# Attention scores on 32-row tiles with the last four dims in a float32r pass, values on 64-column tiles

## The chip, the cores and the metric

The kernel runs on one core of a Trainium2 chip. The metric is the device time of one execution in microseconds (us), the median of several runs.

## The reference

One block of a diffusion transformer on `x` of shape (2, 2048, 576), with a condition vector per batch; 16 heads of 36 dims, hidden layer of 2304. All of it is float32.

```python
mod = jax.nn.silu(c) @ w_ada + b_ada
sh_msa, sc_msa, g_msa, sh_mlp, sc_mlp, g_mlp = jnp.split(mod, 6, axis=1)
xn = _ln(x, 1e-06)
xn = xn * (1 + sc_msa[:, None, :]) + sh_msa[:, None, :]
qkv = (xn @ w_qkv + b_qkv).reshape(B, N, 3, H, hd)
q, k, v = (qkv[:, :, 0], qkv[:, :, 1], qkv[:, :, 2])
q = _ln(q, 1e-05, qn_g, qn_b)
k = _ln(k, 1e-05, kn_g, kn_b)
attn = jnp.einsum('bqhd,bkhd->bhqk', q, k) * scale
attn = jax.nn.softmax(attn, axis=-1)
o = jnp.einsum('bhqk,bkhd->bqhd', attn, v).reshape(B, N, C)
o = o @ w_proj + b_proj
x = x + g_msa[:, None, :] * o
xn2 = _ln(x, 1e-06)
xn2 = xn2 * (1 + sc_mlp[:, None, :]) + sh_mlp[:, None, :]
h = jax.nn.gelu(xn2 @ w1 + b1, approximate=False)
x = x + g_mlp[:, None, :] * (h @ w2 + b2)
```

## The kernel before

The work of one batch goes through three stages, and after both batches the MLP follows.

**Input stage** (`inputs`). For each of 16 tiles of 128 tokens: layer norm, transposes to features by tokens, the product with `w_qkv`, the bias (VectorE), the norm per head, and transposes of q and k back to features by tokens (`by_feature`). Their evictions fill `qo` (the first five 128-row chunks of the 1152 features of q and k) and `kr` (the other four); v stays tokens by features in `vt`, with a column of ones behind every head's 36 columns, so that the values product also sums the softmax's denominator. The contraction over 576 input features is four 128-row tiles (`whole`, line 351) and a rest of 64 rows, which is done for the two output halves side by side on 64-row tiles (`halved`, line 362). In this stage VectorE runs in the order written.

**Attention** (`attend`). Heads go in pairs p (8 of them), queries in blocks qb of 512 (4 of them), keys in chunks kc of 128 (16 of them). For every step (p, qb, kc):
- `scores` (line 900): the 36 dims of a head lie in a 64-row half of `kts[p % 2]` and of `qts`; the rest of the rows is zero. A chunk is cut into two halves of 64 keys, so that two heads times two halves make four products on 64x64 tiles of the TensorE array: keys stationary, 512 queries moving.
- ScalarE takes the exponential of the whole PSUM tile of 128 x 1024 (line 908), into `pt`. There is no maximum to subtract, since a bound on the scores is known from the norms' gains and biases.
- `values` (line 916): the same four tiles, with 64 of the chunk's keys as rows and 64 columns of `vt` as columns. Each of the two key halves has a PSUM bank of its own in `acc`.
- After the last chunk, `finish` adds the two banks (lines 928 and 929, VectorE), writes the row of denominators to DRAM and reads it back broadcast (lines 933 and 934), takes the reciprocal (935), multiplies (936), and puts the rows into `qo` (941), where they replace q.

The loop issues the scores of a step before the values of the step before, so that the exponential of a chunk runs beside TensorE's work on others. PSUM has two tiles of two banks for scores (`s`) and two for `acc`. q and k are brought from `qo` and `kr` to the tiles by SBUF to SBUF DMAs on SyncE's queue (`take_heads`, line 729): two or three for a block of q or a pair of k, as a head's 36 rows lie within one 128-row chunk or across two. There are three q tiles and two k tiles. Each engine's order is made by a scheduler from the program's order and dependencies, so that loads are issued well before the step in which they are written.

The first attention steps of a batch still hold the transposes of the last two token tiles (the hooks at kc 2 and 5 of the first block), whose keys the first block needs in its last four chunks.

**Output projection** (`outputs`) and the **MLP** follow; the change doesn't touch them.

The matmul of a float32 operand is shown in the profile as two records on TensorE (PE) and two weight loads (PEld).

Of the kernel before, what the change touches and what calls it, by code (L numbers as in the profile page):

```python
# [7 lines left out]

F32 = mybir.dt.float32
I32 = mybir.dt.int32  # L10
AF = mybir.ActivationFunctionType
# [10 lines left out]
FULL = 4  # L22
NKC = FULL + 1


@with_exitstack
def dit_block(
# [56 lines left out]
    def acc_tile():  # L84
        return psum["a"].tile([P, 2, 512], F32, tag="acc", name="acc")

# [351 lines left out]
    def attention(b, qk, vt):  # L438
# [4 lines left out]
        with tc.tile_pool(name=f"b1_{b}", bufs=1) as b1p, tc.tile_pool(name=f"b2_{b}", bufs=2) as b2p:  # L443
# [107 lines left out]
            for p in range(NPAIR):  # L551
                behind = None
                for s in range(steps):
                    qb, kc = divmod(s, NT)
                    if kc == 0:
                        qt = shifted_q(p, qb)
                    pt = scores(p, qt, kc)
                    if p + 1 < NPAIR:
                        largest(p + 1, s)
                    if behind is not None:  # L560
                        values(p, *behind)
                        if behind[2] == NT - 1:
                            finish(p, qb - 1, behind[0])
                    if kc == 0:
                        acc = acc_tile()[:, 0, :]
                    behind = (acc, pt, kc)
                    if p + 2 < NPAIR and qb == NBLK - 1 and kc % 2 == 1:
                        prepare(p + 2, kc // 2)
                values(p, *behind)
                finish(p, NBLK - 1, behind[0])  # L570
# [117 lines left out]

    def head_rows(first):

        at = first
        while at < first + HD:
            n = min(P - at % P, first + HD - at)
            yield at // P, at % P, at - first, n
            at += n

    def block_of_small():
# [16 lines left out]
        vv = vt[:, 0 : NT * H * HV].rearrange("p (t h e) -> p t h e", t=NT, h=H)  # L714
        kts = [kv.tile([P, N], F32, name=f"kt{i}") for i in range(2)]
        qts = [kv.tile([P, BLK], F32, name=f"qt{i}") for i in range(3)]
        for t in (*kts, *qts):
            nc.gpsimd.memset(t, 0.0)
        nc.gpsimd.memset(vv[:, :, :, HD : HD + 1], 1.0)
        nc.gpsimd.memset(vt[:, NT * H * HV :], 0.0)  # L720
        den_dram = dram.tile([B, NPAIR, NBLK, 2, BLK], F32, name="den_dram")

        def chunk(c, cols):
            return qo[:, c, cols] if c < NKC else kr[:, c - NKC, cols]

        def take_heads(dst, first, cols):
            for h in range(2):
                for c, row, d, n in head_rows(first + h * HD):
                    nc.sync.dma_start(
                        out=dst[64 * h + d : 64 * h + d + n, :], in_=chunk(c, cols)[row : row + n, :]  # L730
                    )

        def take_k(p, blk=None):
            cols = slice(0, N) if blk is None else slice(blk * BLK, (blk + 1) * BLK)
            take_heads(kts[p % 2][:, cols], C + p * 2 * HD, cols)

        def take_q(p, qb):
            cols = slice(qb * BLK, (qb + 1) * BLK)
            take_heads(qts[(p * NBLK + qb) % 3], p * 2 * HD, cols)

# [36 lines left out]
        def inputs(b, weights, work, xnt, loaded):  # L777

            wq, wq4, bq = weights
            normed, squares = {}, {}  # L780

# [32 lines left out]

            def by_feature(t, parts, all_on_vector=False):
                both = normed.pop(t)
                parts = [
                    parts[c // 8][:, c % 8 // 4, c % 4 * P : c % 4 * P + P] for c in range(NQK)
                ]
                for c, ps in enumerate(parts):  # L820
# [12 lines left out]
                if t % TPB == TPB - 1:  # L833
                    if t == TPB - 1:
                        take_q(0, 0)
                    take_k(0, t // TPB)

# [5 lines left out]
            for t in range(NT):  # L843
                both = work.tile([P, 2 * C], F32, name="both", bufs=3)
                for w in range(3):
# [25 lines left out]
                    if w == (1 if t % 2 == 0 else 0):  # L871
                        if t + 1 < NT:
                            ahead = input_by_feature(b, rows)
                        if t >= 2:
                            by_feature(t - 2, [s_tile(), s_tile()])
                        if t + 2 < NT:
                            rows = next_rows(t + 2)
# [7 lines left out]
                before, xnt = both, ahead  # L885
            return lambda t, spare: by_feature(t, [spare, s_tile()], True)

        def attend(b, pool, hooks):

            def scores(p, qb, kc):
                ps = s_tile()
                for c in range(2):
                    for h in range(2):
                        r = slice(64 * h, 64 * h + 64)
                        k0 = kc * P + 64 * c
                        nc.tensor.matmul(  # L900
                            ps[64 * c : 64 * c + 64, h, :],
                            kts[p % 2][r, k0 : k0 + 64],
                            qts[(p * NBLK + qb) % 3][r, :],
                            start=True,
                            stop=True,
                        )
                pt = pool.tile([P, 2, BLK], F32, name="pt", bufs=3)
                nc.scalar.activation(pt, ps, AF.Exp, scale=SCALE)  # L908
                return pt

            def values(p, acc, pt, kc):
                for h in range(2):
                    for c in range(2):
                        r = slice(64 * c, 64 * c + 64)
                        v0 = (kc * H + 2 * p + h) * HV
                        nc.tensor.matmul(  # L916
                            acc[64 * h : 64 * h + 64, c, :],
                            vt[r, v0 : v0 + 64],
                            pt[r, h, :],
                            start=(kc == 0),  # L920
                            stop=(kc == NT - 1),
                        )

            def finish(p, qb, acc):


                ot = pool.tile([P, BLK], F32, name="ot", bufs=2)
                nc.vector.tensor_copy(ot, acc[:, 0, :])  # L928
                nc.vector.tensor_tensor(ot, acc[:, 1, :], ot, ALU.add)
                den = pool.tile([P, BLK], F32, name="den", bufs=2)  # L930
# [13 lines left out]

            steps = [(p, qb, kc) for p in range(NPAIR) for qb in range(NBLK) for kc in range(NT)]
            behind = None
            for p, qb, kc in [*steps, (None, None, None)]:
                pt = None if p is None else scores(p, qb, kc)
                if (p, qb, kc) in hooks:
                    hooks[p, qb, kc]()  # L950
                if kc == 6 and (p, qb) != (NPAIR - 1, NBLK - 1):
                    take_q(*((p, qb + 1) if qb + 1 < NBLK else (p + 1, 0)))
                if kc == 8 and qb == 1 and p + 1 < NPAIR:
                    take_k(p + 1)
                if behind is not None:
                    bp, bqb, bkc, bpt = behind
                    if bkc == 0:
                        acc = acc_tile()
                    values(bp, acc, bpt, bkc)
                    if bkc == NT - 1:  # L960
                        finish(bp, bqb, acc)
                behind = (p, qb, kc, pt)

# [79 lines left out]
        for b in range(B):  # L1043
# [5 lines left out]
            close_psum()  # L1049
            close_psum = opened_psum(a=2, s=2)  # L1050
            opening = {}
# [24 lines left out]
            def output_opened():  # L1076
# [3 lines left out]
                (0, 0, 0): spare_taken,  # L1080
                (0, 0, 2): lambda: last_inputs(NT - 2, opening["spare"]),
                (0, 0, 5): last_inputs_done,
                (4, 0, 4): output_opened,
            }
            if b == 0:
                hooks |= {
                    (0, 2, 4): ada_opened,
                    (1, 0, 9): ada_gates,
                    (2, 0, 9): ada_feature_rows,
                    (2, 0, 12): ada_features,  # L1090
                }
# [40 lines left out]
        NB = B * NBLK  # L1132
        NG = BLK // PAIR
        gelus = [dram.tile([NG, P, NF, PAIR], F32, name=f"gelu{n}") for n in range(NB)]
        mx, close_mx = opened("mx")
# [176 lines left out]
        def hidden_loaded(q):  # L1312
            n, g = divmod(q, NG)
            nc.sync.dma_start(out=hidden[q % len(hidden)], in_=gelus[n][g])
# [32 lines left out]
        def second_product(q, gate, gate_bias):  # L1347
# [25 lines left out]
            for pair in ((3, 4), (2, 5), (6, 7), (1,)):  # L1373
# [15 lines left out]
                elif pair == (6, 7):  # L1389
                    nc.vector.tensor_tensor(c11, c11, ms[6], ALU.add)  # L1390
                    nc.vector.tensor_tensor(c00, c00, ms[7], ALU.add)
            if q + 3 < NB * NG:
                hidden_loaded(q + 3)
# [8 lines left out]
        for b in range(B):  # L1402
            gate, gate_bias = (hs.tile([P, C], F32, name=f"gate{i}") for i in range(2))
            for i, g in enumerate((gate, gate_bias)):
                nc.sync.dma_start(out=g, in_=gate_dram[2 + i, b, :].partition_broadcast(P))
            for q in range(b * NBLK * NG, (b + 1) * NBLK * NG):
                second_product(q, gate, gate_bias)
# [42 lines left out]
```

## Time and profile before

| | before |
|---|---|
| time, median of 3 | 3492.86 us (3491.9 to 3493.2) |
| span of the profiled execution | 3490.8 us |
| TensorE busy | 3439.7 us, 99% |
| ScalarE busy | 1495.4 us, 43% |
| VectorE busy | 1265.8 us, 36% |
| GpSimd busy | 260.4 us, 7% |
| attention, batch 0 and batch 1 | 265 to 1155 us and 1468 to 2352 us from the span's start |

A group of instructions in the profile is one line of the code, one engine, one operation and one shape. Behind the shapes stand the count, then the group's busy time in us and the mean length of one in ns, and then the idle time of that engine just before these instructions, with what ended most of it. Matmuls on different tiles of the array overlap, so the lengths of their records add to more than the time in which they ran; the distance between starts is what counts. In a timeline the columns are the start, the length of the merged run, the engine, the line, the operation, and the number of instructions; `64*64` is the rows and columns of the array that a matmul uses, and `64x512` its moving operand.

### The profile page before, as it was taken

What the parts mean: (1) busy time and instruction counts of PE and PEld (TensorE: products, weight loads), DVE (VectorE), ACT (ScalarE), POOL (GpSimd) and SP (SyncE); (2) the same over time, 40 slices, a digit from 0 to 9 for tenths busy, and PEclk for the clock granted to TensorE, in tenths of its full rate; (3) what the DMA queues carried; (4) which work ended last, traced back from release to release, by engine and by line L of the source; (5) the groups of instructions that cost most, each with busy time, mean ns of one, the idle gap of its engine ahead of it and who ended that gap; (6) DMA issues with size and microseconds to landing.
All of it is one profiled execution on the core that took longest, in us unless ns stands there. A gap on an engine that the chain in (4) does not pass through costs nothing.

```text
span 3490.8 us, 56258 instructions
## 1 busy us (share of the span) xinstructions
PE 3439.7 (99%) x24287; PEld 1945.6 (56%) x24287; DVE 1265.8 (36%) x1737; ACT 1495.4 (43%) x1928; POOL 260.4 (7%) x250
## 2 busy tenths in 40 slices
PE   8999999999999999999999999998999999999998
PEld 5773333333333677633333333336788788777776
DVE  4662112211121356611121211127445444455554
ACT  2335555555555133355555555551555454000000
POOL 2110000000000111100000000005000000011111
PEclk9999999999999999999999999999999999999999
DMA  3001211111100310011010010015422222433321
GB/s 121 28 21 53 68 50 28 34 29 37 38 22 23 122 36 25 20 46 27 27 29 29 23 28 27 21 37 192 139 99 84 84 86 71 166 122 126 117 104 35
DMA packets 105183, 215.98 MB, mean 62 GB/s; under 512 B 13988, under 2 KB 56557, under 8 KB 101869
## 3 DMA queue, kind: packets, MB, share of 16 engines
q1 hardware_dynamic: 93956, 174.19, 15.6%
q0 software_dynamic: 10240, 36.61, 3.0%
q8 instruction: 193, 3.16, 0.4%
q10 hardware_dynamic: 728, 1.48, 0.2%
q14 instruction: 66, 0.53, 0.1%
HBM read 125.96 MB, written 56.91 MB: 52 GB/s over the span
## 4 chain that ended last, share of the span: by engine, by line
PE 94%; DVE 2%; issue 2%; DMA 1%; ACT 0%; POOL 0%; SPq 0%; DVEq 0%; POOLq 0%; ACTq 0%
PE acc L916 25%; PE s L900 25%; PE s L1378 13%; PE s L351 13%; PE m L1228 11%; PE m L1242 2%; PE s L362 2%; PE one L1228 2%; PE s L821 1%; PE t L1287 1%; PE s L329 0%; DVE xt L259 0%; DMA gb_rows<-rows_dram 0%; DVE x L997 0%; DMA x_dram<-x 0%
## 5 line engine op out<-in xcount | busy, mean ns | idle before, releaser
L908 ACT ACTIVATE pt<-s 128x1024 f32<-128x1024 f32 x1024 | 1048.5, 1024 | 719.5 <-PE s L900 719.5
L916 PE MATMUL acc<-pt,vt 64*64 64x512 f32 x8192 | 1064.5, 589 | 2.4 <-ACT pt L908 2.4
L900 PE MATMUL s<-qt,kt 64*64 64x512 f32 x8192 | 1063.7, 589 | 0.0
L900 PEld LDWEIGHTS s<-qt,kt 64*64 64x64 f32 x8192 | 315.0, 133 | 563.4 <-issue 285.2
L916 PEld LDWEIGHTS acc<-pt,vt 64*64 64x64 f32 x8192 | 309.4, 131 | 570.2 <-ACT pt L908 391.2
L928 DVE COPY ot<-acc 128x512 f32<-128x512 f32 x64 | 44.3, 692 | 1037.0 <-PE acc L916 1037.0
L351 PE MATMUL s<-wq,xnt 128*128 128x288 f32 x1536 | 392.7, 411 | 1.3 <-ACT xnt L337 1.3
L1378 PE MATMUL s<-ws,as 128*128 128x288 f32 x1440 | 351.8, 406 | 0.0
L935 DVE RECIPROCAL den<-den 128x512 f32<-128x512 f32 x64 | 214.6, 3353 | 344.3 <-DMA den<-den_dram 344.3
L351 PEld LDWEIGHTS s<-wq,xnt 128*128 128x128 f32 x1536 | 286.4, 191 | 92.6 <-issue 18.5
L1378 PEld LDWEIGHTS s<-ws,as 128*128 128x128 f32 x1440 | 273.6, 190 | 75.6
L1228 PE MATMUL m<-s,wb 128*128 128x256 f32 x864 | 210.7, 380 | 4.2 <-DVE s L1202 3.2
L1228 PE MATMUL m<-xnt,wb 128*128 128x256 f32 x864 | 214.4, 384 | 0.0
L1228 PEld LDWEIGHTS m<-s,wb 128*128 128x128 f32 x864 | 164.2, 190 | 27.3 <-DVE s L1202 3.6
L1228 PEld LDWEIGHTS m<-xnt,wb 128*128 128x128 f32 x864 | 159.5, 190 | 32.7 <-issue 12.2
L1378 PE MATMUL s<-ws,hidden 128*128 128x288 f32 x576 | 142.3, 406 | 0.0
L1266 ACT ACTIVATE cs<-cs,b_sb 128x512 f32<-128x512 f32 x144 | 103.9, 722 | 87.1 <-DVE cs L1261 87.1
L1364 DVE TENSOR_TENSOR as<-hidden 128x1152 f32<-128x1152 f32 x80 | 139.5, 1808 | 0.0
L337 ACT ACTIVATE xnt<-s,mod 128x128 f32<-128x128 f32 x180 | 66.8, 459 | 159.3 <-PE s L330 147.9
L1255 DVE TENSOR_TENSOR cs<-m,cs 128x512 f32<-128x512 f32 x72 | 49.8, 691 | 235.0 <-ACT cs L1254 157.7
L351 PE MATMUL s<-wp,qo 128*128 128x288 f32 x512 | 130.8, 417 | 0.0
L1378 PEld LDWEIGHTS s<-ws,hidden 128*128 128x128 f32 x576 | 109.4, 190 | 30.2
(142 smaller groups left out, 2069.2 us busy)
## 6 DMA issues: line engine op xcount, KB each, us to landing
gelu<-cs SPq DMA_DIRECT2D x144, 256.0 KB
hidden<-gelu SPq DMA_DIRECT2D x16, 2304.0 KB
den<-den_dram SPq DMA_DIRECT2D x128, 128.0 KB
xr<-x_dram SPq DMA_DIRECT2D x32, 288.0 KB
out_dram<-y POOLq DMA_DIRECT2D x32, 288.0 KB, 3.6
qo<-ot SPq DMA_DIRECT2D x104, 72.0 KB
wa<-in_w_ada_dram SPq DMA_DIRECT2D x12, 576.0 KB
xt<-in_x_dram SPq DMA_DIRECT2D x24, 288.0 KB
```

Source lines behind the costliest of these rows:

```text
L337: nc.scalar.activation(dst[:, k, :], t4[:, k * P : (k + 1) * P] if k < FULL else t1[:, :P], AF.Identity, bias=mod[:, which, k, b : b + 1], ...
L351: nc.tensor.matmul(outs[a], stationary(k, a), moving(k, a), start=(first and k == 0), stop=(not first and k == FULL - 1),)
L362: nc.tensor.matmul(outs[a], stationary(FULL, a)[r], moving(FULL, a)[r], start=first, stop=not first)
L900: nc.tensor.matmul(ps[64 * c : 64 * c + 64, h, :], kts[p % 2][r, k0 : k0 + 64], qts[(p * NBLK + qb) % 3][r, :], start=True, stop=True,)
L908: nc.scalar.activation(pt, ps, AF.Exp, scale=SCALE)
L916: nc.tensor.matmul(acc[64 * h : 64 * h + 64, c, :], vt[r, v0 : v0 + 64], pt[r, h, :], start=(kc == 0), stop=(kc == NT - 1),)
L935: nc.vector.reciprocal(den, den)
L1228: nc.tensor.matmul(out_m[m], wb[:, slot[m], k, f * P : (f + 1) * P], moving[m](k), start=k == 0 and (m == 1 or (first and m in (2, 5, 6))) ...
L1242: nc.tensor.matmul(out_m[m], w[r, f * P : (f + 1) * P], a[r, FULL, t * PAIR : (t + 1) * PAIR], start=first and m != 4, stop=not first and ...
L1266: nc.scalar.activation(part, part, AF.Gelu, bias=b1_sb[:, g : g + 1])
L1364: nc.vector.tensor_tensor(stationary[m], x_, y_, op)
L1378: nc.tensor.matmul(ms[m], stationary[m][:, f, :], ws[m][:, f, :], start=(f == 0), stop=(f == HF - 1))
```

## The change

The scores of a head contract over 36 dims. They are now split in two: 32 dims in float32 on 32-row tiles of the array, of which there are four, and the last 4 dims (`HD - DIMS`) in a second pass in float32r, a reduced type, that adds to the same PSUM tile. For the second pass each of the 4 dims is parted in a high part, which float32r holds, and a low part, the rest. Four copies of the 4 rows (16 rows in all) stand in each 32-row strip; for k they are high, high, low, low, for q high, low, high, low, so that the 16 rows give all four products of the parts.

The four row tiles are two heads times two chunks of keys. A step is now a group g of two chunks: chunk g and chunk g + 8. Keys of the first eight chunks lie in the strips 0 and 1 and those of the last eight in the strips 2 and 3, so that a k tile has half as many columns as before. Each product has 128 key columns and a PSUM bank of its own: a group fills two `s` tiles.

The values contract over all 128 keys of a chunk on two 64-column tiles, one for each head, and add all 16 chunks in one bank; `acc` is now one bank, and the addition in `finish` goes. PSUM now has three `s` tiles and two `acc` tiles.

The rows come by more DMAs: for each strip one or two for its 32 main rows and four for the copies of its last 4. After them VectorE makes the parts (`parted`): two operations on 512 columns. The masks `low_k`, `sign_k` and so on, a column each, say which rows are low. There are two q tiles now, not three, with their own end tiles `qe`, and two of k with `ke`. During the input stage k comes by blocks of 512 (`take_k_block`), and the parting is put into VectorE's written order at the next tile's `by_feature`. The hooks have moved to the groups that stand for about the same steps.

```diff
-    def acc_tile():
-        return psum["a"].tile([P, 2, 512], F32, tag="acc", name="acc")
+    def acc_tile():
+        return psum["a"].tile([P, 512], F32, tag="acc", name="acc")
...
-        kts = [kv.tile([P, N], F32, name=f"kt{i}") for i in range(2)]
-        qts = [kv.tile([P, BLK], F32, name=f"qt{i}") for i in range(3)]
+        km = [kv.tile([P, N // 2], F32, name="km0"), None]
+        qm = [kv.tile([P, BLK], F32, name="qm0"), None]
+        ke = [kv.tile([P, N // 2], F32, name=f"ke{i}") for i in range(2)]
+        qe = [kv.tile([P, BLK], F32, name=f"qe{i}") for i in range(2)]
...
+        high = kv.tile([P, BLK], F32R, name="high")
...
-        def take_heads(dst, first, cols):
-            for h in range(2):
-                for c, row, d, n in head_rows(first + h * HD):
-                    nc.sync.dma_start(
-                        out=dst[64 * h + d : 64 * h + d + n, :], in_=chunk(c, cols)[row : row + n, :]
-                    )
+        def rows_taken(main, ends, halves, first, src, dst):
+            for c in halves:
+                for h in range(2):
+                    r0 = 32 * (2 * c + h)
+                    for i, row, d, n in head_rows(first + h * HD, DIMS):
+                        nc.sync.dma_start(out=main[r0 + d : r0 + d + n, dst], in_=chunk(i, src(c))[row : row + n, :])
+                    ((i, row, _, n),) = head_rows(first + h * HD + DIMS, HD - DIMS)
+                    for j in range(4):
+                        nc.sync.dma_start(
+                            out=ends[r0 + n * j : r0 + n * j + n, dst], in_=chunk(i, src(c))[row : row + n, :]
+                        )
+
+        def parted(ends, rows, low, sign):
+            for a in range(ends.shape[1] // BLK):
+                part = ends[rows, a * BLK : (a + 1) * BLK]
+                nc.vector.tensor_scalar(high[rows, :], part, sign[rows, :], None, ALU.mult)
+                nc.vector.scalar_tensor_tensor(
+                    part.bitcast(F32R), part, low[rows, :], high[rows, :].bitcast(F32), ALU.mult, ALU.add
+                )
...
             def by_feature(t, banks, all_on_vector=False):
                 both = normed.pop(t)
+                while taken:
+                    taken.pop(0)()
...
-            def scores(p, qb, kc):
-                ps = s_tile()
-                for c in range(2):
-                    for h in range(2):
-                        r = slice(64 * h, 64 * h + 64)
-                        k0 = kc * P + 64 * c
-                        nc.tensor.matmul(ps[64 * c : 64 * c + 64, h, :], ...)
+            def scores(p, qb, g):
+                i, j = p % 2, qb % 2
+                keys = slice(g * P, (g + 1) * P)
+                tiles = [s_tile() for c in range(2)]
+                for k, q, first in ((km[i], qm[j], True), (ke[i].bitcast(F32R), qe[j].bitcast(F32R), False)):
+                    for c in range(2):
+                        for h in range(2):
+                            r0 = 32 * (2 * c + h)
+                            r = slice(r0, r0 + (DIMS if first else 4 * (HD - DIMS)))
+                            nc.tensor.matmul(tiles[c][:, h, :], k[r, keys], q[r, :], start=first, stop=not first)
...
+            def values(p, acc, pts, g):
+                for c, pt in enumerate(pts):
                     for h in range(2):
+                        v0 = ((g + c * NT // 2) * H + 2 * p + h) * HV
+                        nc.tensor.matmul(
+                            acc[64 * h : 64 * h + 64, :],
+                            vt[:, v0 : v0 + 64],
+                            pt[:, h, :],
+                            start=(g == 0 and c == 0),
+                            stop=(g == NG - 1 and c == 1),
+                        )
...
-                nc.vector.tensor_copy(ot, acc[:, 0, :])
-                nc.vector.tensor_tensor(ot, acc[:, 1, :], ot, ALU.add)
+                nc.vector.tensor_copy(ot, acc)
...
-            close_psum = opened_psum(a=2, s=2)
+            close_psum = opened_psum(a=2, s=3)
```

## The prediction

> **What bounds the kernel now.** I read the page's shares and chain first.
>
> ```profile
> PE 3439.7 (99%) x24287; PEld 1945.6 (56%) x24287; DVE 1265.8 (36%) x1737; ACT 1495.4 (43%) x1928; POOL 260.4 (7%) x250
> PE 94%; DVE 2%; issue 2%; DMA 1%; ACT 0%; POOL 0%; SPq 0%; DVEq 0%; POOLq 0%; ACTq 0%
> ```
>
> TensorE sets the end; L916 and L900, the two attention lines, carry 25% of the chain each. Next the groups with their shapes kept apart.
>
> ```profile
> L916 PE MATMUL acc<-pt,vt 64*64 64x512 f32 x8192 | 1064.5, 589 | 2.4 <-ACT pt L908 2.4
> L900 PE MATMUL s<-qt,kt 64*64 64x512 f32 x8192 | 1063.7, 589 | 0.0
> L908 ACT ACTIVATE pt<-s 128x1024 f32<-128x1024 f32 x1024 | 1048.5, 1024 | 719.5 <-PE s L900 719.5
> ```
>
> 1024 chunks with 4 products on each line make 4096 matmuls but 8192 records: a float32 matmul is two records. The timeline of the middle of attention gives the pace:
>
> ```profile
> 1001.68 1.04 PE L916 MATMUL acc<-pt,vt 64*64 64x512 f32 x8
> 1002.54 1.04 PE L900 MATMUL s<-qt,kt 64*64 64x512 f32 x8
> 1003.40 1.04 PE L916 MATMUL acc<-pt,vt 64*64 64x512 f32 x8
> ```
>
> Eight records start every 0.858 us, so the four tiles run side by side, in two waves of 0.429 us (one for each record of a float32 matmul). Two chunks cost 4 x 0.858 = 3.432 us. There are 512 such pairs (2 batches x 8 head pairs x 4 query blocks x 8), together 1757 us of 3493. ScalarE needs 2 x 1.024 us in that time and has room.
>
> What a change of tile shape costs is seen where the timeline crosses one: first between 128-row and 64-row tiles in the input stage, then from 128x128 transposes to 64x64 tiles.
>
> ```profile
> 55.53 0.65 PE L351 MATMUL s<-wq,xnt 128*128 128x288 f32 x2
> 56.11 1.24 PE L362 MATMUL s<-wq,xnt 64*128 64x288 f32 x8
> 57.28 2.45 PE L351 MATMUL s<-wq,xnt 128*128 128x288 f32 x9
> ...
> 267.72 1.09 PE L916 MATMUL acc<-pt,vt 64*64 64x512 f32 x8 [0.96 <-ACT pt L908]
> 268.63 1.04 PE L900 MATMUL s<-qt,kt 64*64 64x512 f32 x8
> ```
>
> A 288-column record normally takes 0.243 us. From 55.53 two of them would end at 56.02; L362 starts at 56.11, 0.09 late. Its 8 records are four waves of two, 0.97 us, but L351 comes 1.17 us later: 0.20 more, 0.10 for the first weights and 0.10 for the way back. The first L351 record then again waits some 0.10 for weights (128 columns). With 64-column weights the first wave loses only 0.05: 267.72 to 268.63 is 0.91, not 0.858. So a switch costs 0.093 us plus an exposed weight load of 0.105 (128 columns) or 0.05 (64 columns).
>
> Column tiles with all 128 rows do run side by side: the modulation products are 40 records, ten waves of four, in 2.97 us.
>
> ```profile
> 394.07 3.03 PE L177 MATMUL s<-wa,sil 128*32 128x320 f32 x40
> 397.04 1.09 PE L916 MATMUL acc<-pt,vt 64*64 64x512 f32 x8
> ```
>
> Last, the DMA queue of SyncE, since the change multiplies its issues. The three numbers are shortest, median and longest issue in ns; below them is one query block.
>
> ```profile
> L729 SPq DMA_DIRECT2D qt<-qo x160: 564/722/1592, 109.5 to 2268.5; - x160
> ...
> 576.17 2.05 SPq L729 DMA_DIRECT2D qt<-qo  x3
> 580.25 0.51 SPq L933 DMA_DIRECT2D den_dram<-ot  x2
> 581.38 1.13 SPq L934 DMA_DIRECT2D den<-den_dram  x2
> 588.98 1.62 SPq L941 DMA_DIRECT2D qo<-ot  x2
> ```
>
> The queue is busy about 5.3 us in a block of 27.5 us (8 x 3.432).
>
> [...]
>
> **The change part by part.** The unit is a group of two chunks, 512 of them.
>
> - Scores, 32 dims: four 32-row matmuls (two chunks x two heads), 128 columns wide, each in a row tile and a PSUM bank of its own. If they run side by side as the four 64x64 tiles do, that is two waves: 2 x 0.429 = 0.858 us, where two chunks took 1.716.
> - Scores, last 4 dims: four float32r matmuls on the same row tiles.[...] upper end, if the moving operand goes at the pace of one float32 record, 0.429 us. I take 0.216[...]. Their weights can load during the second float32 wave.
> - Values: the contraction is over 128 rows, so two column tiles run together, not four. Four matmuls are two pairs of two waves: 4 x 0.429 = 1.716 us, as before.
> - Switches: before there is none between scores and values (both 64x64). Now there are two per group: 0.093 + 0.105 into the scores, 0.093 + 0.051 into the values; the staggered starts (7 ns a tile) add 0.028. Together 0.370 us.
>
> New group: 0.858 + 0.216 + 1.716 + 0.370 = 3.160 us against 3.432: 0.272 us less, x 512 = 139 us.
>
> - ScalarE: 2.05 us of exps in 3.16. The values of a group wait for exps that ended some 0.9 us earlier; the next scores need the third s tile and the one that the first exp frees, about 1.3 us after scores end, while 1.87 us of values lie between. Hidden.
> - VectorE: the eviction loses one 0.69 us addition and gains two operations to part q (nearest rows: 0.69 us each), and four per head pair for k. It is 36% busy. Hidden behind TensorE unless its inputs come late.
> - SyncE: q for a block takes 20 or 22 DMAs (4 to 6 of main rows, 16 of four rows each), not 2 or 3; k for a head pair 20 to 22. In the built instruction order the loads for block b+2 start after block b's last scores, since buffers are two; the denominators of block b queue behind some 16 of them, and VectorE's reciprocal stands ahead of the parting. I walked this order with 0.65 us per issue (the 32-row qt issues of before take 0.565, a 4-row one 0.62, plus 0.05 between) and 2 us to land (the denominator read: issue ended 328.4, reciprocal began 330.9). q is parted some 21 us after its load begins and needed after 27. SyncE is busy 105 x 0.65 + 14 = 82 us of the 101 us of a head pair. Blocks that also load k run late by a few us: 8 us in all. At 0.75 us per issue the same walk gives 37 us per batch, at 0.60 none.
> - Start of attention: the last key block passes the transposes of tile 15, evictions (0.4 us each), 11 DMAs (7 us), 2 us to land and 1.4 us of parting: ready 22 us after the first scores. The fifth group, which needs it, comes at 13 us (before: the thirteenth chunk, at 23). A stall of 8.5 us, twice: 17.
> - Input stage: block 0 of q and k is 31 DMAs, 20 us; VectorE parts it one tile later (a tile takes 15 us), and everything behind it on VectorE, the bias additions that empty TensorE's tiles first, waits. Four PSUM tiles cushion this: 2 us a batch, 4.
> - The MLP and projection are untouched: nothing.
>
> Sum: 3492.9 - 139 + 8 + 17 + 4 = 3383.
>
> **The rivals.**
> - Dear float32r: the pass takes 0.429 us[...]. For: nothing in the trace shows the pass.[...] +0.213 x 512 = 109, less the 8 of queue stalls: 3484, about where it was.
> - SyncE becomes the bound: 0.75 us per issue (36-row issues are at the median of 0.72), stalls of 37 us per batch: 3383 + 74 - 8 = 3449. Against: most new issues have four rows.
> - Cheaper switches: with weights preloaded across them, 0.156 x 512 = 80 us less: 3303. Against: every crossing in the trace shows the load.
> - Slower: the float32r tiles run one after another, 4 x 0.216 in place of one, +0.648 x 512 = 332: 3715. Against: float32 row tiles L362 start 7 ns apart; for: a different type, not seen.
>
> **How the numbers follow.** Forecast 0.58, dear float32r 0.14, SyncE 0.13, cheaper switches 0.08, serial tiles 0.07. The likeliest gives 3383. The range leaves out the serial tiles and the cheapest switches, and runs from 3330 (half of those switches' gain, with few stalls) to 3488 (float32r at its upper end). Faster takes the first, third, fourth and two thirds of the second: 0.88; the rest of the second is split into same, 0.03, and slower, 0.02, to which the serial tiles add 0.07: 0.09.
>
> **What would show it.** In the trace after, groups should start every 3.16 us. Scores records should come in two waves of 0.43 us and one of 0.22; values in four waves of 0.43, the first near 0.48. About 0.09 us should lie extra at either edge of the scores. TensorE should wait some 8 us for VectorE's parting of k early in each attention stage, and a few us in one block per head pair. A group near 3.37 us means dear float32r; idle time at every block's start means SyncE; float32r records 0.2 us apart mean serial tiles. The prediction is wrong if TensorE's waves do not keep these counts.

## The result and the profile after

The changed kernel takes 3378.18 us (median of 4 runs, 3374.95 to 3382.14) against 3493.03 (4 runs): a ratio of 0.9672, 95% interval 0.9655 to 0.9688. The forecast was 3383.

The first lines are the page's busy times and the chain of waits of the changed kernel.

```profile
PE 3318.8 (98%) x18143; PEld 1839.6 (54%) x18143; DVE 1313.8 (39%) x1877; ACT 1439.7 (43%) x1928; POOL 258.8 (8%) x249
PE 93%; DVE 2%; issue 2%; SPq 1%; DMA 1%; ACT 1%; POOL 0%; DVEq 0%; POOLq 0%; ACTq 0%
```

TensorE still sets the end. It has 6144 records less (18143 after 24287); SyncE's queue has come into the chain with 1%. The groups of attention, shapes kept apart:

```profile
L968 PE MATMUL acc<-pt,vt 128*64 128x512 f32 x4096 | 996.2, 607 | 0.0
L956 PE MATMUL s<-qm,km 32*128 32x512 f32 x4096 | 592.3, 641 | 3.6 <-DMA km<-kr 1.4
L956 PE MATMUL s<-qe,ke 16*128 16x512 f32 x2048 | 419.9, 789 | 8.2 <-DVE ke L762 5.1
```

The 8192 records of values became 4096 (one matmul over 128 keys in place of two over 64). The 8192 of scores became 4096 for 32 dims, two for each float32 matmul, and 2048 for the last 4 dims: a float32r matmul is one record. That group has the longest waits of the two lines, 8.2 us, most of it for VectorE's parting (line 762).

The timeline of TensorE in the middle of attention, from one group of two chunks to the next:

```profile
1001.80 1.14 PE L956 MATMUL s<-qm,km 32*128 32x512 f32 x8
1002.36 0.82 PE L956 MATMUL s<-qe,ke 16*128 16x512 f32 x4
1003.11 1.94 PE L968 MATMUL acc<-pt,vt 128*64 128x512 f32 x8
1004.98 1.14 PE L956 MATMUL s<-qm,km 32*128 32x512 f32 x8
```

From scores to scores it is 3.18 us here. Over the trace, groups of 3.168 and of 3.175 us alternate, with a median of 3.171, where two chunks took 3.433. The scores with both their passes take 1.31 us (1001.80 to 1003.11) and the values 1.87.

The matmul starts of the two traces, put together by stage:

| stage | before, us | after, us | difference |
|---|---|---|---|
| input, batch 0 | 255.4 | 257.5 | +2.1 |
| attention, batch 0 | 889.8 | 836.5 | -53.3 |
| projection and input, batch 1 | 313.7 | 318.3 | +4.6 |
| attention, batch 1 | 882.8 | 824.4 | -58.4 |
| last projection and MLP | 1129.6 | 1122.5 | -7.1 |

The pace makes 512 x (3.433 - 3.171) = 134 us less. Attention as a whole lost only 111.7, so that some 22 us more than before are spent off the pace. The last row was not foreseen: no line of that code was changed. (The two profiled executions lie 110.5 us apart, the medians of the runs 115.)

**Off the pace.** At the start of attention the fifth group waits for the last key block. The timeline of all engines of the changed kernel there:

```profile
284.12 2.47 SPq L753 DMA_DIRECT2D ke<-kr  x4
287.88 0.49 DVE L761 TENSOR_SCALAR high<-ke,part 64x512 fp32r<-64x512 f32 x1 [7.96 <-DMA ke<-kr]
288.41 0.75 DVE L762 SCALAR_TENSOR_TENSOR ke<-ke,part,high 64x512 fp32r<-64x512 f32 x1
289.21 0.97 PE L956 MATMUL s<-qe,ke 16*128 16x512 f32 x2 [2.12 <-DVE ke L762]
290.11 2.80 PE L968 MATMUL acc<-pt,vt 128*64 128x512 f32 x6
```

The copies are issued one after another, 0.62 us each, VectorE waits for them, TensorE for VectorE. The last line tells something else: six records of values take 2.80 us where eight took 1.94. The granted clock was 0.5 for 6.8 us from 285.9 on. From its first scores to those of the next group (282.44 to 293.27), the group that holds this takes 7.65 us more than the pace, in batch 1 8.22.

The same happens in the middle, in a block that also loads k. Timelines of SyncE's queue, VectorE and TensorE:

```profile
419.64 5.09 SPq L753 DMA_DIRECT2D qe<-qo  x8
424.83 0.66 SPq L984 DMA_DIRECT2D den_dram<-ot  x2
...
431.09 3.35 DVE L986 RECIPROCAL den<-den 128x512 f32<-128x512 f32 x1 [19.89 <-DMA den<-den_dram]
435.61 0.75 DVE L762 SCALAR_TENSOR_TENSOR qe<-qe,part,high 128x512 fp32r<-128x512 f32 x1
436.41 1.22 PE L956 MATMUL s<-qe,ke 16*128 16x512 f32 x4 [2.67 <-DVE qe L762]
437.56 3.68 PE L968 MATMUL acc<-pt,vt 128*64 128x512 f32 x8
```

The denominators came late: VectorE had copied them out of PSUM by 411.2, but their DMAs queue behind the copies of q and went out at 424.83. The reciprocal ahead of the parting holds it up, the last 4 dims of the scores wait 2.67 us, and the values after them take 3.61 us (to the next scores at 441.17) instead of 1.87.

### The profile page after: what moved, and what is told of

Read it like the earlier page. It is cut to its first block, busy times and chain, and to the rows that moved or that the text cites. A ratio compares the mean times of both kernels' runs of the same rounds, so it can differ in the third digit from the quotient of the medians.

```text
span 3380.3 us, 46567 instructions
## 1 busy us (share of the span) xinstructions
PE 3318.8 (98%) x18143; PEld 1839.6 (54%) x18143; DVE 1313.8 (39%) x1877; ACT 1439.7 (43%) x1928; POOL 258.8 (8%) x249
## 4 chain that ended last, share of the span: by engine, by line
PE 93%; DVE 2%; issue 2%; SPq 1%; DMA 1%; ACT 1%; POOL 0%; DVEq 0%; POOLq 0%; ACTq 0%
PE acc L968 28%; PE s L956 20%; PE s L1431 14%; PE s L356 13%; PE m L1281 11%; PE m L1295 2%; PE s L367 2%; PE one L1281 2%; SPq L753 1%; PE s L866 1%; PE t L1340 1%; PE s L334 0%; DVE xt L264 0%; DMA wa<-in_w_ada_dram 0%; PE s L182 0%
## 5 line engine op out<-in xcount | busy, mean ns | idle before, releaser
L960 ACT ACTIVATE pt<-s 128x1024 f32<-128x1024 f32 x1024 | 992.6, 1021 | 664.7 <-PE s L956 664.6
L968 PE MATMUL acc<-pt,vt 128*64 128x512 f32 x4096 | 996.2, 607 | 0.0
L956 PE MATMUL s<-qm,km 32*128 32x512 f32 x4096 | 592.3, 641 | 3.6 <-DMA km<-kr 1.4
L968 PEld LDWEIGHTS acc<-pt,vt 128*64 128x64 f32 x4096 | 249.4, 136 | 578.3 <-issue 576.5
L956 PE MATMUL s<-qe,ke 16*128 16x512 f32 x2048 | 419.9, 789 | 8.2 <-DVE ke L762 5.1
L956 PEld LDWEIGHTS s<-qm,km 32*128 32x128 f32 x4096 | 162.4, 183 | 423.6 <-PE acc L968 262.9
L356 PEld LDWEIGHTS s<-wq,xnt 128*128 128x128 f32 x1536 | 286.5, 191 | 95.1 <-issue 18.5
L956 PEld LDWEIGHTS s<-qe,ke 16*128 16x128 f32 x2048 | 109.4, 186 | 127.3 <-issue 113.0
```

The lines of the kernel that those rows point to most:

```text
L356: nc.tensor.matmul(outs[a], stationary(k, a), moving(k, a), start=(first and k == 0), stop=(not first and k == FULL - 1),)
L956: nc.tensor.matmul(tiles[c][:, h, :], k[r, keys], q[r, :], start=first, stop=not first)
L968: nc.tensor.matmul(acc[64 * h : 64 * h + 64, :], vt[:, v0 : v0 + 64], pt[:, h, :], start=(g == 0 and c == 0), stop=(g == NG - 1 and c == 1),)
```

## Experiments

Theory: the gain is the pace alone, made of terms that can be taken apart (two waves, one float32r pass, four waves, two switches), and what was given back is the number of small DMAs on SyncE's queue. Rivals: the float32r pass or the change of type is dear and something else pays for it; the stalls come from the work of parting, not from the DMAs.

**One part alone: values on 64-column tiles.** The kernel before, one chunk per step, with the values of the change.

```diff
-                for h in range(2):
-                    for c in range(2):
-                        r = slice(64 * c, 64 * c + 64)
-                        ... acc[64 * h : 64 * h + 64, c, :], vt[r, v0 : v0 + 64], pt[r, h, :]
+                for h in range(2):
+                        ... acc[64 * h : 64 * h + 64, 0, :], vt[:, v0 : v0 + 64], pt[:, h, :]
```

> The kernel before with one part of the change: values over 128 rows on two 64-column tiles in one bank, scores on 64x64 tiles as they were, one chunk per step. Theory: the values cost as much as before, two waves of two pairs, 0.858 us a chunk, but every chunk now has two switches of 0.093 + 0.05 us and 0.03 us of stagger: 1024 x 0.32 = 324 us more, near 3817. Rival (two column tiles are no worse than four tiles and switches are cheap): within 60 us of 3493.

3806.82 us. A chunk takes 2.028 us where it took 1.717: +0.311. The matmul time is the same by count, so this is what two switches with 64-column weights cost. By itself this part loses 312 us (3494.47 beside it); what it brings is the tiles of 128 keys that the four row tiles need.

**The second pass in float32.** The last 4 dims as they are, four rows, no copies and no parting.

```diff
-    for k, q, first in ((km[i], qm[j], True), (ke[i].bitcast(F32R), qe[j].bitcast(F32R), False)):
+    for k, q, first in ((km[i], qm[j], True), (ke[i], qe[j], False)):
...
-                    for j in range(4):
+                    for j in range(1):
...
```

> The last 4 dims in float32 in place of float32r: four rows, no copies and no parting, the same result. Theory: the pass becomes two waves of 0.43 us in place of one of 0.22, so the group is 3.17 + 0.64 = 3.81 us, 512 x 0.64 = 329 us more, less some 18 us of waits that fewer DMAs take away: near 3690, above the kernel before by about its two switches a group (0.37 x 512 = 189 us). Rival (the gain is from row tiles and the float32r pass matters little): within 60 us of 3378.

3674.13 us, a group of 3.798 us:

```profile
1002.01 1.14 PE L951 MATMUL s<-qm,km 32*128 32x512 f32 x8
1002.97 1.04 PE L951 MATMUL s<-qe,ke 4*128 4x512 f32 x8
1003.94 1.94 PE L963 MATMUL acc<-pt,vt 128*64 128x512 f32 x8
1005.81 1.14 PE L951 MATMUL s<-qm,km 32*128 32x512 f32 x8
```

The pass costs 3.798 - 3.171 = 0.627 more than in float32r. Two float32 rounds on row tiles at 0.858 and the values at 1.716 make 3.432; what is above that, 0.366, is the two switches. The forecast had 0.370. The projection and input stage between the batches took 316.0 us here, 318.3 with the copies and 313.7 before.

**No second pass at all.** The float32r matmuls are left out, 32 of 36 dims are scored; the loads and the parting stay.

```diff
-    for k, q, first in ((km[i], qm[j], True), (ke[i].bitcast(F32R), qe[j].bitcast(F32R), False)):
-        for c in range(2):
-            for h in range(2):
-                ...
+    for c in range(2):
+        for h in range(2):
+            r = slice(32 * (2 * c + h), 32 * (2 * c + h) + DIMS)
+            nc.tensor.matmul(tiles[c][:, h, :], km[i][r, keys], qm[j][r, :], start=True, stop=True)
```

> The changed kernel without the float32r matmuls: the scores are of 32 dims only, so the last 4 dims are missing from them; their DMAs and the parting stay. Theory: the pass costs one pass of 512 columns, about 0.22 us of the 3.17 us group, and no type switch: 512 x 0.22 = 113 us less, near 3265 us, group 2.95 us. Rival (dear float32r, 0.43 us[...]): some 220 us less, near 3160.

3488.53 us: a miss by 223. The group's median is 2.938 us, near the 2.95 expected, yet attention took 889.0 and 878.7. The largest item of TensorE's waits, then the queue of SyncE and TensorE at one of them:

```profile
PE s L954 <- DMA qm<-qo: 75.7, 23, 9.1
```

```profile
793.53 13.86 SPq L753 DMA_DIRECT2D qe<-qo  x22
...
809.55 4.58 PE L954 MATMUL s<-qm,km 32*128 32x512 f32 x8 [6.05 <-DMA qm<-qo]
```

With no matmul that reads `qe`, the loads of `qe` are free early, and the scheduler put 22 of them in a row ahead of the `qm` that TensorE needs. The wait of 6.05 us is followed by scores of 4.58 us instead of 1.14, while the last rows of q still arrive (their loads are issued from 808.77 to 810.57). Three more waits, 50.4 us together, stand under VectorE's work for the modulation; in one of them VectorE itself waits 18.5 us for denominators whose DMAs were issued behind 23 loads of `qe`. So this run shows nothing of the pass's price on the whole time, but a good deal about the queue. For that the order of the loads has to stay as it was.

**The second pass in two groups of eight.** So the float32r matmuls stay in the first and last group of each block and are left out between (there, 32 of 36 dims are scored).

```diff
+    short = g not in (0, NG - 1)
+    if first or not short:
-    nc.tensor.matmul(tiles[c][:, h, :], k[r, keys], q[r, :], start=first, stop=not first)
+        nc.tensor.matmul(tiles[c][:, h, :], k[r, keys], q[r, :], start=first, stop=short or not first)
```

> The changed kernel with the float32r pass only in the first and the last group of each query block; the other six groups take scores of 32 dims only. The end tiles keep a reader in every block, so the loads keep their order. The pass takes 0.23 us away from six groups of eight: 89 us less, 3289, if nothing else binds. Theory (SyncE's queue is near its limit, 82 us of work in a head pair that now lasts 95): waits for q and k of 25 to 60 us, 3315 to 3350, more still where a long wait lowers the clock. Rival (the queue has room, and the waits of the run without the pass came from the moved loads alone): 3285 to 3300.

3318.80 us. Its timeline shows a group with the pass and one without:

```profile
1000.14 1.14 PE L958 MATMUL s<-qm,km 32*128 32x512 f32 x8
1000.70 0.81 PE L958 MATMUL s<-qe,ke 16*128 16x512 f32 x4
1001.44 1.94 PE L972 MATMUL acc<-pt,vt 128*64 128x512 f32 x8
1003.31 1.14 PE L958 MATMUL s<-qm,km 32*128 32x512 f32 x8
1004.38 1.94 PE L972 MATMUL acc<-pt,vt 128*64 128x512 f32 x8
```

1.30 us of scores against 1.07. By the medians, 3.171 - 2.938 = 0.233 us is the whole price of the pass, its change of type included. The quicker groups leave SyncE less room, though:

```profile
PE s L958 <- DVE qe L762: 19.0, 11, 2.9
```

Eleven waits of 19.0 us in all, where the changed kernel had two of 3.1. Only some 58 of the 384 x 0.233 = 89 us came through: the queue is close to its limit.

**One DMA for the four copies.** The source is read four times by one DMA; the rows of a strip then stand dim by dim, and the masks follow.

```diff
-                    for j in range(4):
-                        nc.sync.dma_start(
-                            out=ends[r0 + n * j : r0 + n * j + n, dst], in_=chunk(i, src(c))[row : row + n, :]
-                        )
+                    rows = chunk(i, src(c))[row : row + n, :]
+                    nc.sync.dma_start(
+                        out=ends[r0 : r0 + 4 * n, dst],
+                        in_=rows.unsqueeze(1).to_broadcast([n, 4, rows.shape[1]]),
+                    )
```

> The changed kernel with the four copies of the last 4 rows brought by one DMA (a source read four times over), so that q takes 8 or 10 DMAs, not 20 or 22, and k the same; the masks follow the new order of the rows. Theory (the waits early in each attention stage and in blocks that load k come from SyncE's queue, 0.64 us an issue): the wait for the last key block shrinks from some 6 us to 2 or none, twice, those of the first blocks vanish, the input stage gets 4 back: 18 to 28 us less, 3350 to 3360, groups at 3.17 us as before. Rival (those waits come from the evictions and VectorE's order, and the queue was never late): within 5 us of 3378.

The changed kernel was timed again beside it:

> The changed kernel unaltered, on the same chip as the next three: 3378 us within 5.

The changed kernel again: 3376.84 us, ratio 0.967 (0.9656 to 0.9683). With one DMA: 3359.26 us (3357.45 to 3362.55), ratio 0.962 (0.9607 to 0.9633). It beats both kernels, the changed one by 17.6 us. The pace is the same, 3.17. By the two profiles, 9.2 us of the difference are in attention of batch 0, 2.3 in that of batch 1, 3.7 between the batches, 1.4 in the first input stage and 1.0 behind attention. The start of attention, VectorE and TensorE:

```profile
284.35 0.49 DVE L762 TENSOR_SCALAR high<-ke,part 64x512 fp32r<-64x512 f32 x1 [5.70 <-DMA ke<-kr]
285.68 0.55 PE L957 MATMUL s<-qe,ke 16*128 16x512 f32 x2 [1.65 <-DVE ke L763]
286.15 3.54 PE L969 MATMUL acc<-pt,vt 128*64 128x512 f32 x8
```

The parting is the same work. It starts 17.6 us after the first scores, at 284.35; in the changed kernel it was 19.9 us. The waits in the blocks that load k are gone, so there the number of DMAs, and not VectorE's parting, made the stalls. At the starts it made the smaller part: from scores to scores, 5.28 us are left in batch 0 and 6.44 in batch 1, where the changed kernel, in its second profile, has 8.06 and 7.97. So the forecast of this run, 2 us or none at each start, missed there. What is left, from the transposes' evictions to the landing of the remaining DMAs, was not taken apart. The half clock stays for a shorter time in batch 0: from 267 to 300 us the mean granted clock is 0.95 here and 0.90 in the changed kernel.

**Both together.** One DMA for the copies, and the second pass in two groups of eight (the other groups score 32 of 36 dims).

> The same as the run before, with one DMA for the four copies: the float32r pass in two groups of eight only. Theory: the queue has room again, so the 89 us come whole: the one-DMA kernel's time less 89, near 3265. Rival (the waits come from elsewhere, VectorE's order or ScalarE): the time stays above 3300.

3266.55 us: 3359.26 less 93. Some 8 of these come at the starts, where the fifth group has no second pass now and doesn't wait for parted keys; the other 85 are nearly all of the 89. TensorE's waits for the parting of q are gone.

**Four switches instead of two.** The values of the first chunk go between the 32-dim scores and the float32r pass, those of the second behind the pass.

```diff
+               tiles = None if p is None else [s_tile() for c in range(2)]
+               scores(p, qb, g, True, tiles)
+               values(bp, acc, bpts, bg, 0)
-               pts = scores(p, qb, g)
+               pts = scores(p, qb, g, False, tiles)
...
-               values(bp, acc, bpts, bg)
+               values(bp, acc, bpts, bg, 1)
```

> The same matmuls in another order: 32 dims of a group, then the values of one chunk, then the float32r pass, then the values of the other chunk: four changes of tile shape per group, not two. Theory[...]: 0.37 us more per group, 189 us in all, near 3567. Rival (a switch costs only what the weights cost, or is hidden): under 90 us more.

3665.68 us, about 100 more than expected. TensorE's timeline:

```profile
1000.88 1.38 PE L955 MATMUL s<-qm,km 32*128 32x512 f32 x8
1002.20 1.08 PE L969 MATMUL acc<-pt,vt 128*64 128x512 f32 x4
1003.21 0.51 PE L955 MATMUL s<-qe,ke 16*128 16x512 f32 x4
1003.65 1.08 PE L969 MATMUL acc<-pt,vt 128*64 128x512 f32 x4
1004.65 1.38 PE L955 MATMUL s<-qm,km 32*128 32x512 f32 x8
```

The group is 3.77 us here; the median over the trace is 3.748, +0.577. The values take 1.01 and 1.00 us and the pass 0.44, 0.14 to 0.21 more in each than their waves (0.858, 0.858, 0.233): the switches as expected. The surplus is in the first part: 1.32 us here, 1.29 in the median, instead of 1.07. Its second pair of row tiles starts 0.23 us (median) after the first, and 0.05 us after the exponential that holds its `s` tile ends (1001.09 here), for the scores now come back sooner than ScalarE frees the third tile. So this wait is ScalarE's, as far as the trace shows; the remaining 0.34 is what two switches cost.

**The stretch behind attention.** The 7 us there appear in no line of the diff. In the kernel before, GpSimd's timeline at the start of the last projection is:

```profile
2350.85 2.84 POOL L981 DMA_DIRECT2D x<-in_x_dram  x5 [879.47 <-ACT pt L908]
2370.14 0.54 POOL L981 DMA_DIRECT2D x<-in_x_dram  x1 [16.45 <-DMA qo<-ot]
2370.69 4.14 POOL L985 TENSOR_TENSOR x<-x,gate 128x576 f32<-128x576 f32 x3
```

and in the changed kernel:

```profile
2248.73 1.59 POOL L1032 DMA_DIRECT2D x<-in_x_dram  x3 [1.78 <-issue]
2250.34 4.13 POOL L1036 TENSOR_TENSOR x<-x,gate 128x576 f32<-128x576 f32 x3
```

Before, the sixth residual load waits 16.45 us for the last write back of attention, and the additions stand behind it in GpSimd's order. VectorE and then TensorE wait for them: 4.64 and 4.13 us in two waits, against one of 3.96 after (of 1.2 in the second profile of the changed kernel, so this one differs from execution to execution). The theory is that the sixth residual buffer lies in memory that attention's output tile had, and that the change, which gives attention other tiles, moved it. To try this, two of the twelve residual buffers are exchanged in the kernel before, and nothing else.

```diff
+        x1_tiles = [scratch.tile([P, C], F32, name=f"x1_{i}") for i in range(12)]
+        x1_tiles[5], x1_tiles[11] = x1_tiles[11], x1_tiles[5]
-        outputs(B - 1, wp, between, [scratch.tile([P, C], F32, name=f"x1_{i}") for i in range(12)])
+        outputs(B - 1, wp, between, x1_tiles)
```

> The kernel before, with two of the twelve residual buffers of the last projection exchanged, so that the sixth residual load writes another piece of memory; nothing else differs. Theory: the sixth load waited 16.45 us because its buffer lies where an output tile of attention had been, whose write back landed late; GpSimd's order then held the first additions, and TensorE twice waited for VectorE and went on at half clock. With another buffer the load goes out at once, the stretch behind attention takes 1117 to 1123 us as in the changed kernel instead of 1128 to 1130, and the time is 6 to 12 us below the kernel before: 3481 to 3487. Rival: the 7 us come from something else (where the memory traffic of the MLP falls, or scatter): the load may go out early but the time stays within 2 us of 3493.

3484.01 us (3481.65 to 3485.42) against 3494.54 (3491.87 to 3497.01), ratio 0.9968 (0.9956 to 0.998).

```profile
2351.75 3.37 POOL L981 DMA_DIRECT2D x<-in_x_dram  x6 [879.47 <-ACT pt L908]
```

All six loads go out in a row, TensorE's two waits shrink to 0.32 and 1.60 us, and the stretch takes 1120.6 us. So where this buffer lies is worth 10.5 us in the kernel before. In the changed kernel no residual load of this stage waits for a write back of attention either, and the stretch is 7 to 12 us shorter than before (1129.6 to 1122.5 in its first profile, to 1117.8 in its second). That these 7 to 12 us of the 115 have the same cause, and nothing to do with scores, is read from the traces; the opposite exchange was not tried in the changed kernel.

## Why the prediction was right

- **Scores, 32 dims, and values.** Foreseen 0.858 and 1.716, with the switches 2.944 for a group without the float32r pass. Measured 2.938 in the run without it. The row tiles run four at once, the column tiles two at once: in the changed kernel four records of scores start together at 1001.80, and of the values two at 1003.59 and two at 1004.02.
- **The float32r pass.** Foreseen 0.216, with 0.429 as the upper end. Measured 0.233, about a quarter of the 0.858 of a float32 round; in float32 the same pass took 0.627 more. The 0.216, half of a float32 record's 0.43, was the author's assumption: the trace of the kernel before has no float32r operation. What a change of type between float32 and float32r on the same row tiles costs by itself was not shown; it is within the 0.233.
- **Switches.** Foreseen 0.370 for a group. Measured 0.366 in the run with a float32 second pass, and 0.311 with 64-column weights on both sides, for which the same terms give 2 x (0.093 + 0.051) = 0.288 and a stagger. The terms fit these sums; how a switch divides into the 0.093 and the first weights no run here shows by itself.
- **Group.** 3.160 against 3.171: 134 us instead of 139.
- **ScalarE and VectorE hidden.** Right in the changed kernel; nothing of attention's steady pace waits for the exponential. The run with four switches shows how near the third `s` tile is to not being enough.
- **Stalls inside attention.** Foreseen 8 in blocks that load k and 17 at the starts, 25 in all. Counted from scores to scores, so that the slow values behind a stall are in it, the starts are 7.65 and 8.22 + 0.59, or 16.5, and the blocks with a visible wait 5.40 + 0.84, 1.27, 0.67 and 0.18, or 8.4: 24.9 in all. (The stage table makes some 22 of it, since the edges of a stage, where scores or values stand alone, are 1.3 us shorter against the pace than before.) The walk of the queue was right too: the last keys were parted 21.2 us after the first scores (foreseen 22), and the group that needs them came at 14.5 (13). Two things were not as foreseen. Not every head pair has a block that waits, but four blocks in all. And a stall is not a pure wait: of the first one TensorE waits some 3 us, and the rest is row tiles that run two at a time as their keys arrive, and half clock (0.5 from 285.9 to 292.7), which the forecast did not have. That the sums agree so closely is in part luck.
- **Issue time.** Foreseen 0.65 us for each DMA of four rows; eight in a row took 5.09, or 0.636.
- **Input stage.** Foreseen 4; measured 2.1 + 4.6. Of the 4.6, 3.7 go with the four copies, as the run with one DMA has 314.6.
- **MLP and projection.** Foreseen nothing; 7.1 us less. Here the forecast failed, by looking at the diff's lines and not at what a changed set of tiles does to the memory that later tiles take. With -134, +22.3, +6.7, -7.1 and 1.6 us of a later start and end the spans' difference of 110.5 is complete. The forecast had the same 110 through small misses that cancel, and that part of its closeness is luck: 5 us too much hoped of the pace, 2.7 too little set aside for the input stages and nothing for the later start, against 2.7 too much for the stalls and the 7 here.

The rivals: dear float32r and serial tiles fall with 0.233 us; cheaper switches with 0.366. SyncE as the bound was wrong for this pace but not far: 0.233 us less in six groups of eight was enough to bring eleven waits.

## What to carry to other kernels

When a product's contraction doesn't fill its tiles, count the waves: a shape that saves waves may pay for two changes of tile shape per group, which cost 0.37 us here. A group must hold enough work for that: with two changes for every single chunk, the values' new shape alone lost 312 us. Count the DMAs too: 0.64 us of queue time for each small copy turned into waits of TensorE, and one DMA that reads its source four times gave 17.6 us back. When tiles are added or taken away, read the trace where the next stage begins; a buffer that lay on another's memory cost 10.5 us here.

## What the runs showed of the hardware

A short wait can cost more than itself, where the granted clock falls to half. In the middle of attention TensorE waited 2.67 us, and the values after it took 3.61 us instead of 1.87, at a granted clock of 0.5. In the changed kernel's attention the clock fell to 0.5 at 285.9, 436.1 and 1443.0 us, each time for 6.8 us; the other stretches at 0.5 in the traces of the kernels before and after, except the last of each, at the end of the execution, took 3.41 or 6.83 us. In the 4 us before the three falls TensorE was idle for 0.82, 2.37 and 2.55 us. In the first of these the larger wait, 2.12 us, came after the fall; before it TensorE had work for two of its four row tiles at a time (six records of scores in 2.27 us, where eight take 1.14). With one DMA for the copies, a wait of 1.65 us at the start of attention was followed by values of 3.47 us, with a mean granted clock of 0.95 from 267 to 300 us. Which share of work keeps the clock up was not measured. The extreme was the run without the second pass: a mean granted clock of 0.962, against 0.993, with 23 waits for q.

A DMA of q's rows occupies SyncE's queue for 0.585 us (median) with 4 rows, and for 0.666 with 4 rows read four times: so in these two runs the time goes with the issue and hardly with the rows.
